# Six buffers of exponentials taken strictly in turn

## The chip, the cores and the metric

The kernel runs on one core of one Trainium2 chip. The metric is the device time in microseconds of that core, the median of three runs; lower is better.

## What is computed

The input x is 4 images of 128 channels and 64 x 64 positions, in float32. Two layers are applied. The first is a deformable 3 x 3 convolution. The second treats the 4096 positions of an image as tokens of 128 values, and has attention with 16 heads of 8 values, a small feed-forward part, and a mixture of 8 experts of which each token uses two. Cut to what matters here, the second layer is:

```python
x = x + deform_conv(group_norm(x), ...)            # layer 0
t = tokens(x)
heads = layer_norm(t).reshape(Bs, Ss, H, D)        # H = 16, D = 8
q = transpose(ring(heads + rx_theta), (0, 2, 1, 3))
scores = einsum('bhsd,bhtd->bhst', q, q) / sqrt(D)
attn = softmax(scores, axis=-1)
ctx = einsum('bhst,bhtd->bhsd', attn, q)
...                                                # projection, feed-forward, experts
```

Queries, keys and values are one and the same tensor q, so the matrix of scores is symmetric.

## The kernel before

Attention is the bulk of the work. An image has 8 chunks of 512 positions (NCH), each chunk has 4 tiles of 128 keys, and the 16 heads form 4 groups of 4 (NGRP). A *run* is one group of heads with one chunk of 512 queries; it goes over its tiles t of 128 keys. One (run, t) is a *step*. There are 3700 steps.

A step has these parts:

- `scores` (L1241): four matmuls (L1249), one a head, put the transposed scores of 128 keys and 512 queries into two PSUM tiles of the tag "sc", two heads in each. The pool of "sc" has three buffers. Two activations on ScalarE (L1258), one a PSUM tile, write the exponentials into two SBUF tiles named e, 128 x 1024 float32 each. Tag "e" has six buffers.
- `context` (L1262): the matmuls of L1266 multiply the two tiles e with the values qf (which carry a column of ones for the softmax sums) and add up in the PSUM tile acc, over all steps of a run. At the end of a run acc is copied to cu (L1468, L1470) and stored.
- `turn` (L1134): because the scores are symmetric, the exponentials of one block of queries and keys can serve, transposed, for another run. The steps that give such blocks are in the set `gives`. For them VectorE transposes both tiles e into a tile st (L1140), from where SyncE stores them to DRAM (etd, L1150). There are 396 such steps, with 792 transposes. The taking run loads them as et (L1184) and its matmuls are L1202.

So a tile e is read by PE (L1266), and in a given step by VectorE (L1140) as well. The buffer of e comes free when both are done.

The order of the main loop (L1401) is: scores of step n + 2 are issued (LAG is 2) as soon as step n is at hand; `turn` for steps n and n + 1; then a portion of the other work; then `context` of step n. On PE the scores of step s therefore stand after the context of step s - 3 and before that of step s - 2. The other work (preparing the next image, whose gathers run on GpSimd and whose convolution matmuls are L275 from L748; finishing earlier chunks with projection, feed-forward and experts) is cut into small pieces by generators. A planner, the class `Beside` (L62), puts them between the steps by its own clock of costs and due times.

The program order is kept as written for PE, VectorE, SyncE and GpSimd:

```python
with tc.manual_schedule(engines={PE, DVE, SP, POOL}):
```

ScalarE is not in that list. Its instructions are ordered, and the buffers of each tag handed out, when the program is built: the builder plays the program through and gives a tile one of the buffers of its tag that it holds to be free by then. Each instruction then gets semaphore waits for whatever its buffer's last readers are. VectorE's buffers that matter here are st (three, also used for tr, the transposed samples on their way to the DRAM table smd, L685 and L697), and v for the gathered samples.

Of the kernel before, what the change touches and what calls it, by code (L numbers as in the profile page):

```python
# [9 lines left out]
F32 = mybir.dt.float32  # L10
# [12 lines left out]
P = 128  # L23
# [195 lines left out]
def kernel(  # L219
# [29 lines left out]
    work = ctx.enter_context(tc.tile_pool(name="work", bufs=2))  # L249
# [162 lines left out]
    for i in range(NFX):  # L412
        t = big.tile([P, 4, QR], F32, name=f"fx{i}")
# [819 lines left out]
    def load_queries(run):  # L1233
        b, g, sc = runs[run][:3]
        if run not in queries and (b, sc) in prepared:
# [2 lines left out]
            queries[run] = q  # L1238
            landing[run] = beside.now + 4.0

    def scores(run, t):  # L1241
        b, g = runs[run][:2]
        ps = [
            ps_s.tile([P, 2, 512], F32, tag="sc", name=f"sc{run}_{t}_{pr}") for pr in range(2)
        ]
        kT, qT = keys[b, g, t // 4][0], queries[run]
        for i in range(4):
            h = 32 * i
            nc.tensor.matmul(  # L1249
                ps[i // 2][:, i % 2, :],  # L1250
                lhsT=kT[h : h + 32, P * (t % 4) : P * (t % 4 + 1)],
                rhs=qT[h : h + 32, :],
                start=True, stop=True,
            )
        es = []
        for pr in range(2):
            e = work.tile([P, 2, 512], F32, tag="e", name=f"e{run}_{t}_{pr}", bufs=6)
            nc.scalar.activation(e, ps[pr], AF.Exp, scale=1.0 / math.sqrt(HD))  # L1258
            es.append(e)
        return es  # L1260
# [133 lines left out]
    with tc.manual_schedule(engines={PE, DVE, SP, POOL}):  # L1394
# [6 lines left out]
        while n < len(steps):  # L1401
            if issued < len(steps) and issued <= n + LAG and at_hand(issued, n):
                es.append(scores(*steps[issued]))
                issued += 1
            elif issued <= n:
                if beside.has("prepare"):
                    beside.force("prepare")
                else:
                    beside.now += beside.STEP
                    beside.flush(beside.now)  # L1410
                continue
            run, t = steps[n]
# [137 lines left out]
```

## Time and profile before

| What | Value |
|---|---|
| Time, median of 3 runs | 7758.01 us (7747.74 to 7768.12) |
| The profiled execution's own time | 7722.51 us |
| Its span, first to last instruction | 7720.7 us |
| Mean granted TensorE clock | 0.966 |
| PE, ScalarE, VectorE, GpSimd busy | 93%, 89%, 58%, 21% of the span |
| Activations of L1258 | 7400 |
| Transposes of L1140 | 792 |

The profile is of one execution. PE is TensorE, PEld its weight loads, ACT ScalarE, DVE VectorE, POOL GpSimd, SP SyncE. Matmuls are pipelined and their ends are modelled, so a busy PE is not one at its peak. A group of instructions is named by its line, engine, operation, and the tiles that it writes and reads (acc<-e,qf), with buffer numbers left out. Behind a bar stands the time for which the engine was idle just before the group's instructions, and what ended most of that. In the list of waits a row reads: the waiting instructions, an arrow, whose end released them; then the total in us, the number of times, and the longest. In the timeline, rows run by start time; neighbours of the same line are merged, with a count.

### The profile page before, as it was taken

The page shows a single profiled execution, that of the slowest core. Times are in us where ns is not written, and L with a number is a line of the kernel's source. Part 1 is how long each engine was busy: PE and PEld are TensorE (multiplying, and loading weights), DVE is VectorE, ACT ScalarE, POOL GpSimd, SP SyncE. Part 2 cuts the span into 40 slices and gives each one's busy share as a digit, 9 for nine tenths or more (in the row PEclk, how much of TensorE's full clock was granted, in tenths as well). Part 3 has the DMA queues.
Part 4 walks back from the last instruction along what each step waited for, and adds up shares of the span by engine and source line. Part 5 has one row for each costly group of instructions (what it writes and reads, how often), then busy time and mean ns, then how long its engine had stood idle before and what let it go on. Part 6 is the DMA issues. An engine that isn't in the chain of part 4 may idle for free.

```text
span 7720.7 us, 181988 instructions
## 1 busy us (share of the span) xinstructions
PE 7154.7 (93%) x73736; PEld 2520.7 (33%) x73736; DVE 4480.6 (58%) x8976; ACT 6870.4 (89%) x7441; POOL 1655.8 (21%) x1326
## 2 busy tenths in 40 slices
PE   3589899899999999999999989989999999999997
PEld 2122233223333333333333323333333333333333
DVE  6766356666444767776444677765444545545444
ACT  0578899788999899999999988989999999999995
POOL 5544034443001332422000334431000000000000
PEclk6789999999999999999999999999999999999998
DMA  6677477978557878887766788998665587777762
GB/s 182 206 224 225 135 221 240 286 246 284 155 164 212 264 238 268 281 269 240 211 173 192 237 251 286 286 299 248 187 187 160 150 253 242 246 237 253 240 216 75
DMA packets 922615, 1730.71 MB, mean 224 GB/s; under 512 B 169074, under 2 KB 393356, under 8 KB 871084
## 3 DMA queue, kind: packets, MB, share of 16 engines
q1 hardware_dynamic: 821918, 1412.48, 60.2%
q0 software_dynamic: 92160, 302.06, 12.1%
q8 instruction: 579, 9.49, 0.5%
q10 hardware_dynamic: 7694, 4.52, 0.2%
q14 instruction: 264, 2.16, 0.1%
HBM read 1059.11 MB, written 659.57 MB: 223 GB/s over the span
## 4 chain that ended last, share of the span: by engine, by line
PE 80%; DMA 7%; DVE 4%; issue 3%; ACT 3%; SPq 2%; another core or an unknown queue 0%; POOL 0%; ACTq 0%; POOLq 0%; DVEq 0%
PE acc L1266 39%; PE sc L1249 23%; PE acc L1202 5%; PE conv_ps L275 4%; PE e_ps L275 3%; ACT e L1258 3%; PE f_ps L275 2%; DMA et<-etd 2%; DMA sT<-smd 1%; DMA etd<-st 1%; PE om_ps L530 1%; DVE v L642 1%; DVE st L1140 0%; PE ao_ps L275 0%; DMA qT<-qTd 0%
## 5 line engine op out<-in xcount | busy, mean ns | idle before, releaser
L1258 ACT ACTIVATE e<-sc 128x1024 f32<-128x1024 f32 x7400 | 6867.2, 1068 | 712.8 <-PE sc L1249 456.0
L1266 PE MATMUL acc<-e,qf 128*32 128x512 f32 x29600 | 3957.2, 605 | 18.5 <-DVE cu L1468 11.7
L1249 PE MATMUL sc<-qT,kT 32*128 32x512 f32 x14800 | 2386.7, 499 | 256.0 <-ACT e L1258 158.9
L1249 PEld LDWEIGHTS sc<-qT,kT 32*128 32x128 f32 x14800 | 954.9, 183 | 3655.4 <-ACT e L1258 3087.5
L622 POOL DMA_INDIRECT v<-tab,idx x1152 | 1453.5, 1262 | 1739.0 <-DVE tr L685 1095.4
L1140 DVE STREAM_TRANSPOSE st<-e 128x1024 f32<-128x1024 f32 x792 | 937.7, 1222 | 793.3 <-ACT e L1258 590.3
L1266 PEld LDWEIGHTS acc<-e,qf 128*32 128x32 f32 x29600 | 800.9, 110 | 580.4 <-issue 332.6
L390 POOL TENSOR_TENSOR r<-ln_t,expo 128x4 f32<-128x4 f32 x96 | 112.2, 1169 | 3134.4 <-DVE ln_t L388 3086.5
L642 DVE TENSOR_TENSOR v<-v,wt 128x1536 f32<-128x1536 f32 x384 | 665.8, 1734 | 101.3 <-DMA v<-tab,idx 78.8
L1202 PE MATMUL acc<-et,qf 128*32 128x128 f32 x12672 | 519.8, 281 | 36.4 <-DMA et<-etd 30.5
L1064 DVE TENSOR_TENSOR eo<-e_ps,gt 128x512 f32<-128x512 f32 x256 | 175.1, 686 | 546.9 <-PE e_ps L275 536.6
L1202 PEld LDWEIGHTS acc<-et,qf 128*32 128x32 f32 x12672 | 301.7, 109 | 235.2 <-issue 185.2
L275 PE MATMUL conv_ps<-sT,wconv_sb 128*32 128x256 f32 x4320 | 354.5, 401 | 25.0 <-DMA sT<-smd 19.4
L647 DVE TENSOR_TENSOR v<-v 128x768 f32<-128x768 f32 x384 | 367.4, 957 | 9.7
L1468 DVE COPY cu<-acc 128x512 f32<-128x512 f32 x128 | 88.5, 691 | 392.5 <-PE acc L1266 340.7
L685 DVE STREAM_TRANSPOSE tr<-v 128x128 f32<-128x128 f32 x1080 | 249.4, 282 | 33.1 <-DMA etd<-st 19.9
L648 DVE TENSOR_TENSOR v<-v 128x384 f32<-128x384 f32 x384 | 215.7, 562 | 13.3
L390 POOL TENSOR_TENSOR rstd<-lt_t,expo 128x4 f32<-128x4 f32 x32 | 55.7, 1741 | 523.2 <-DVE lt_t L388 514.2
L275 PE MATMUL f_ps<-w_sb,h 128*32 128x128 f32 x4096 | 165.1, 280 | 0.0
L949 DVE TENSOR_SCALAR h<-h_ps,b_sb 128x512 f32<-128x512 f32 x128 | 94.9, 743 | 102.2 <-PE h_ps L947 97.5
L822 POOL COPY fx<-rn 128x512 f32<-128x512 f32 x32 | 29.5, 923 | 531.4 <-DVE rn L821 333.8
L275 PEld LDWEIGHTS conv_ps<-sT,wconv_sb 128*32 128x32 f32 x4320 | 86.4, 109 | 162.0 <-issue 152.1
(224 smaller groups left out, 3079.3 us busy)
## 6 DMA issues: line engine op xcount, KB each, us to landing
etd<-st SPq DMA_DIRECT2D x1584, 256.0 KB
et<-etd SPq DMA_DIRECT2D x396, 1024.0 KB
kT<-kTd SPq DMA_DIRECT2D x400, 256.0 KB
smd<-tr SPq DMA_DIRECT2D x360, 192.0 KB
sT<-smd SPq DMA_DIRECT2D x360, 192.0 KB
qf<-fqd SPq DMA_DIRECT2D x400, 144.0 KB
qT<-qTd SPq DMA_DIRECT2D x166, 256.0 KB
atd<-cu SPq DMA_DIRECT2D x128, 256.0 KB
```

Of the source, the lines that this page charges most:

```text
L275: nc.tensor.matmul(dst[c : c + 32], lhsT=lhsT[:, c : c + 32], rhs=rhs, start=start, stop=stop)
L622: nc.gpsimd.indirect_dma_start(out=v[:, k, :], out_offset=None, in_=tab, in_offset=bass.IndirectOffsetOnAxis(ap=idx[:, j, kk : kk + 1], ax ...
L642: nc.vector.tensor_tensor(v4, v4, w12[:, :, None].to_broadcast([P, 12, C]), ALU.mult)
L647: nc.vector.tensor_tensor(v[:, :, : 2 * C], v[:, :, : 2 * C], v[:, :, 2 * C :], ALU.add)
L648: nc.vector.tensor_tensor(v[:, :, :C], v[:, :, :C], v[:, :, C : 2 * C], ALU.add)
L685: nc.vector.transpose(out=tr9[:, k, :, j % 4, :], in_=v[:, k, :C].rearrange("p (c i) -> p c i", i=32),)
L1064: nc.vector.tensor_tensor(ws[hf], pe.rearrange("p (e c) -> p e c", c=C), gt[:, i, 4 * hf : 4 * (hf + 1), None].to_broadcast([P, 4, C]), AL ...
L1140: nc.vector.transpose(out=st[:, :, 2 * pr : 2 * pr + 2, :].rearrange("p o h (q j) -> p o (h q) j", j=32), in_=es[pr].rearrange("p h (q o i ...
L1202: nc.tensor.matmul(acc[32 * h : 32 * (h + 1), P * kt : P * (kt + 1)], lhsT=qf[:, t, QW * h : QW * h + 32], rhs=e[:, :, h, 32 * t : 32 * (t ...
L1249: nc.tensor.matmul(ps[i // 2][:, i % 2, :], lhsT=kT[h : h + 32, P * (t % 4) : P * (t % 4 + 1)], rhs=qT[h : h + 32, :], start=True, stop=True,)
L1258: nc.scalar.activation(e, ps[pr], AF.Exp, scale=1.0 / math.sqrt(HD))
L1266: nc.tensor.matmul(acc[32 * h : 32 * (h + 1), :], lhsT=qf[:, t % 4, QW * h : QW * h + 32], rhs=es[h // 2][:, h % 2, :], start=(t == ts[0]) ...
```

## The change

A counter is kept over all tiles e. Each tile gets a tag of its own name, "e0" to "e5", by the counter modulo six, and each of the six tags has one buffer. So the tile at count k always lies where the tile at count k - 6 lay, which is three steps earlier and the same half of the step. The amount of SBUF is the same. Nothing else is changed.

```diff
+    weights_made = [0]
+
     def scores(run, t):
...
         es = []
         for pr in range(2):
-            e = work.tile([P, 2, 512], F32, tag="e", name=f"e{run}_{t}_{pr}", bufs=6)
+
+            e = work.tile([P, 2, 512], F32, tag=f"e{weights_made[0] % 6}", name=f"e{run}_{t}_{pr}", bufs=1)
+            weights_made[0] += 1
             nc.scalar.activation(e, ps[pr], AF.Exp, scale=1.0 / math.sqrt(HD))
             es.append(e)
         return es
```

## The prediction

> **What bounds the kernel now.** I read the page first, then ScalarE's waits, then two stretches of the timeline. On the page, parts 1 and 5 show two engines near their limit:
>
> ```profile
> PE 7154.7 (93%) x73736; PEld 2520.7 (33%) x73736; DVE 4480.6 (58%) x8976; ACT 6870.4 (89%) x7441; POOL 1655.8 (21%) x1326
> L1258 ACT ACTIVATE e<-sc 128x1024 f32<-128x1024 f32 x7400 | 6867.2, 1068 | 712.8 <-PE sc L1249 456.0
> ```
>
> The exponentials are 7400 activations, two a step, 3700 steps. The columns behind the bars are busy time, mean of one, and idle time ahead. ScalarE runs from 178 to 7637 us with little else than these, so what ends its 712.8 us of waits is the question. ScalarE's waits (total, times, longest):
>
> ```profile
> ACT e L1258 <- PE sc L1249: 456.0, 182, 122.5
> ACT e L1258 <- PE acc L1266: 148.5, 138, 2.7
> ...
> ACT e L1258 <- DVE st L1140: 10.7, 4, 4.9
> ```
>
> The first row is true supply: the scores were late. The second should not exist. An exponential reads scores, not acc. It can wait for the context matmul (L1266) only because that matmul still reads the buffer which the exponential is to overwrite. In PE's order, scores of step s are put down after the context of s-3 and before that of s-2. Six buffers in turn hold three steps, so the last PE reader of a buffer in turn is the context of s-3, ahead of the very scores that the exponential waits for. These 138 waits therefore mean a buffer used again after two steps. The third row is VectorE's transposes, the other reader, for the steps that are "given".
>
> The timeline shows the price. First an undisturbed step, with eight convolution matmuls beside it (columns: start, length, engine, line, operation, count, idle time before and its releaser):
>
> ```profile
> 3369.78 10.41 ACT L1258 ACTIVATE e<-sc 128x1024 f32<-128x1024 f32 x11 [0.28 <-PE sc L1249]
> ...
> 3371.11 0.50 PE L1249 MATMUL sc<-qT,kT 32*128 32x512 f32 x4
> ...
> 3371.55 0.64 PE L275 MATMUL conv_ps<-sT,wconv_sb 128*32 128x256 f32 x8
> ...
> 3372.01 1.04 PE L1266 MATMUL acc<-e,qf 128*32 128x512 f32 x8
> ...
> 3372.98 0.51 PE L1249 MATMUL sc<-qT,kT 32*128 32x512 f32 x4
> ```
>
> The step takes 3372.98 - 3371.11 = 1.87 us and ScalarE never stops: eleven activations in 10.41 us. Ten microseconds later, the same work:
>
> ```profile
> 3382.47 1.94 ACT L1258 ACTIVATE e<-sc 128x1024 f32<-128x1024 f32 x2 [1.36 <-PE acc L1266]
> 3383.54 0.19 PEld L1249 LDWEIGHTS sc<-qT,kT 32*128 32x128 f32 x2 [1.05 <-ACT e L1258]
> 3383.54 0.49 PE L1249 MATMUL sc<-qT,kT 32*128 32x512 f32 x2 [0.75 <-ACT e L1258]
> ...
> 3385.56 1.94 ACT L1258 ACTIVATE e<-sc 128x1024 f32<-128x1024 f32 x2 [1.15 <-PE acc L1266]
> 3386.63 0.18 PEld L1249 LDWEIGHTS sc<-qT,kT 32*128 32x128 f32 x2 [1.05 <-ACT e L1258]
> ```
>
> 3386.63 - 3383.54 = 3.09 us a step. It is a ring: the exponential waits for the context, the second scores wait for the exponential to empty their PSUM, the next context stands behind those scores. PE and ScalarE take turns, and both lose.
>
> **What the Trainium skill says.** "Perfetto Trace Analysis", Optimization Strategy: a gap that repeats on the engine that should be saturated can mean that there is no buffer for the next tile. The 1.15 us gaps above agree, though here six buffers are enough and the wrong one is taken. Same page, Identifying Dependency Chains: an instruction with waits on several engines may get EventSemaphore instructions ahead of it. The trace has 7393 of them, 17 ns each, before 7400 activations, so one more waiting condition adds at most such an instruction. "TensorE: Matmul & The Clock Gate", What's actually happening: an idle window of about 3.4 us halves the PE clock. The trace agrees: after a 4.28 us stop at 1713.5 us the eight context matmuls take 1.93 instead of 1.06 us.
>
> **The change, part by part.** Instructions, DMAs and their order on PE, VectorE, SyncE and GpSimd stay. Names and a counter cost nothing on the chip. Only waits of the exponentials change.
>
> *Removed:* the 138 waits on acc, 148.5 us, mean 1.08. All lie on the ring, so on the path. A second price: 3.09 - 1.87 = 1.22 us a step, times 138, is 168. A step without other matmuls gives less (2.66 at 1703 us against 1.83 at 4812 us: 0.83). I take 148.5 and keep 168 as the upper end. What is late next is PE itself, at 1.87 us a step beside 1.81 for two activations (their median spacing is 0.904).
>
> *Added:* strict turns forbid stepping around a buffer that VectorE still reads. I set the end of each of the 792 transposes (396 steps) against the start, in this trace, of the activation six places later. In 385 steps the transpose ends first: nothing is added. In eleven it ends later, by 0.05 to 9.6 us, 38.6 us together; about 1.1 us more each once the acc wait ahead is gone: 51 us. All eleven are late for a store or a load out of VectorE's own buffers:
>
> ```profile
> DVE st L1140 <- DMA etd<-st: 58.8, 14, 11.4
> DVE st L1140 <- DMA smd<-tr: 55.9, 10, 11.6
> ```
>
> But most of it was being paid already. The worst place:
>
> ```profile
> 1702.95 1.94 ACT L1258 ACTIVATE e<-sc 128x1024 f32<-128x1024 f32 x2 [0.72 <-PE acc L1266]
> ...
> 1711.12 2.37 DVE L1140 STREAM_TRANSPOSE st<-e 128x1024 f32<-128x1024 f32 x2 [11.38 <-DMA etd<-st]
> ...
> 1712.46 2.15 ACT L1258 ACTIVATE e<-sc 128x1024 f32<-128x1024 f32 x2 [4.90 <-DVE st L1140]
> ```
>
> Before, ScalarE did two more steps on short-turned buffers and then stood 4.90 us for this very transpose. After, it stands two steps earlier until the same 1712.4 and has those steps still to do: 2 x 1.86 = 3.7 us lost, not 9.4. I went through all eleven so. In seven a PE wait of 1.0 to 3.5 us on VectorE or a DMA follows within 12 us (g_ps, e_ps, conv_ps, et), and takes up the delay. The twenty short-turned steps there, worth 23.5 us in the 148.5, then bring 2.4 us lost instead: take off 26. Behind a standing activation are queued only later activations; PE waits for those two scores later.
>
> *Given back later:* after 1000 us PE's stops that do not end on an exponential are only 119 us; five follow such a stretch within 30 us outside the eleven, and eat about 1.2 us each: 6.
>
> *Unknown:* the stretches concerned have the DMA engines at 0.84 to 0.88 of their time (1000 to 1900, 2500 to 3600, 4400 to 5300 us, where 146 of the 148.5 us lie) and the same transfers must fit in 5% less. More stores will be late, each a stop of ScalarE, some long enough to halve the clock. Lower bound a gain of 10.7 us: earlier exponentials let the transposes and their stores start earlier, which can take away no more than the st row that ScalarE has now. Upper bound a loss of 89 us: the 114.7 us of the two rows above, each a stop of ScalarE in full, less the 26 counted. I take 24 lost, nearer the low end, because VectorE is only about 70% busy there and its stores start when exponentials end, so they move forward too.
>
> Sum: -148.5 + 26 + 6 + 24 = -92 us. The profiled execution took 7722.5 us (span 7720.7 and 1.8 around it), so 7630, or -1.2%. The median of the runs shown is 7758.0, 0.5% above the profiled one; the same share gives 7666.
>
> **The rivals.** (A) As above, 40 to 150 us gained. (B) The DMA engines pace the stretches: what the exponentials save comes back as stops for stores and loads, at the upper bound above: 148.5 - 26 - 6 - 89 = 27 us remain, 7731. For it: DMA shares of 0.93 to 1.00 in pieces such as 1310 to 1400 or 3110 to 3155 us. Against it: so few PE stops on DMA. (C) Slower: VectorE holds buffers and ScalarE can no longer step around. If all DMA-ended waits ahead of the transposes (164 us in the view of tile st) stop ScalarE in full and half the saving is lost otherwise, 164 - 74 = 90 us more: 7848. It decides once stops for VectorE sum to more than what the acc waits gave, that is above 0.4 us on the mean of 396 given steps; the trace has 0.1 now. (D) The buffers were in turn already, and nothing changes: 7758. The 138 waits speak against it.
>
> **How the numbers follow.** A 0.68, B 0.23, C 0.06, D 0.03. About 0.3% (23 us) is what a measurement here can tell from no change. A is faster throughout; half of B is over the bound: 0.83 faster, 0.11 same, 0.06 slower. The range goes from 7612 (146 us gained: the price of 168 with 26 and 6 off and 10.7 on) to 7732, the upper bound of the unknown; it leaves out C, D and a part of B.
>
> **What would show it.** The row of exponentials on acc L1266 should vanish, to below 10 us. The row on st L1140 should rise from 10.7 to 40 to 80. Steps of 3.09 us at 3380 us should be 1.87. PE's and ScalarE's busy shares rise a point. It is wrong if waits on acc remain (then the reuse was not their cause), if st L1140 exceeds 150 us, or if PE's stops on et, conv_ps and sT grow by as much as acc gave.

## The result and the profile after

The changed kernel takes 7828.32 us, median of 4 runs (7827.28 to 7845.88). The kernel before takes 7753.91 us over 4 runs that were made beside them. The ratio is 1.0100, interval 1.0086 to 1.0114: slower, where -1.2% was forecast. The profiled execution took 7845.9 us, with a span of 7844.1 against 7720.7 us and a mean granted clock of 0.959 against 0.966. The two profiled executions lie further apart (123 us) than the medians (74 us): the one after is the slowest of its four, and the one before is 25 us faster than any timed run of its kernel. So the traces are read for what grew and where, not for the exact size of the loss.

These are the lines of the page after that answer to those shown of before. The change added lines to the file, so the exponentials are now L1262, their scores L1251, the context matmuls L1270.

```profile
PE 7223.7 (92%) x73736; PEld 2526.2 (32%) x73736; DVE 4481.1 (57%) x8976; ACT 6880.9 (88%) x7441; POOL 1654.9 (21%) x1326
L1262 ACT ACTIVATE e<-sc 128x1024 f32<-128x1024 f32 x7400 | 6877.8, 1065 | 824.8 <-PE sc L1251 626.8
```

The work is the same in number and nearly in length. What grew is the idle time ahead of the exponentials, from 712.8 to 824.8 us. That is 112 us of the 123.4 by which the span grew; 10.6 more is their busy time (6877.8 against 6867.2). Next, ScalarE's waits in the changed kernel (total, times, longest):

```profile
ACT e L1262 <- PE sc L1251: 626.8, 377, 122.1
ACT e L1262 <- issue: 104.1, 21, 70.7
...
ACT e L1262 <- PE acc L1202: 14.8, 11, 2.6
...
ACT e L1262 <- DVE st L1140: 5.9, 4, 2.4
```

The row on acc L1266 (now L1270), 148.5 us before, is gone without a remainder. The row on st L1140, which was to rise to 40 to 80 us, fell from 10.7 to 5.9. The scores' row rose from 456.0 us in 182 waits to 626.8 in 377. One stop has changed its name and has to be put back first. It lies near the start, ends in the first row below in the kernel before and in the second in the kernel after, and is as long in both:

```profile
296.39 5.61 ACT L1258 ACTIVATE e<-sc 128x1024 f32<-128x1024 f32 x6 [70.64 <-PE sc L1249]
...
293.47 5.61 ACT L1262 ACTIVATE e<-sc 128x1024 f32<-128x1024 f32 x6 [70.68 <-issue]
```

Before, it is in the scores' row; after, it is the longest of the row "issue". Like for like, the scores' row grew from 456.0 to 697.5 us, by 241.5. So the change did take away the wait that it could take away. A larger wait for scores came up, and waits for VectorE have no part in it.

PE shows the other half. These are the rows of the context matmuls on the page before and on the page after:

```profile
L1266 PE MATMUL acc<-e,qf 128*32 128x512 f32 x29600 | 3957.2, 605 | 18.5 <-DVE cu L1468 11.7
...
L1270 PE MATMUL acc<-e,qf 128*32 128x512 f32 x29600 | 4026.2, 608 | 70.2 <-ACT e L1262 46.0
```

The idle time ahead of them grew from 18.5 to 70.2 us. PE now stops ahead of contexts because an exponential is missing, for 46.0 us, and ScalarE stops because scores are missing. Each waits for the other, though both have the same amount of work as before.

**The order on ScalarE.** A wait for scores that grows while nobody computes scores later suggests that ScalarE asks for other scores than PE delivers. So the two programs were compared, instruction by instruction. On PE, VectorE, SyncE and GpSimd the order is the same. On ScalarE it is not. Before, all 7400 exponentials stand in the order in which they are written. After, 293 of them stand elsewhere, at 60 places. The place that the timeline below shows reads thus (place among the 7400 exponentials, counted from 0, then the tile e of run, key tile and half):

```
before: 3004 e88_15_0, 3005 e88_15_1, ..., 3010 e88_29_0, 3011 e88_29_1, 3012 e88_30_0, 3013 e88_30_1, ...
after:  3004 e88_15_0, 3005 e88_15_1, ..., 3010 e88_30_0, 3011 e88_30_1, ..., 3014 e88_29_0, 3015 e88_29_1
```

The step of key tile 29 stands three steps behind that of key tile 15 and must take its two buffers. Key tile 15 is a given step: VectorE transposes those buffers too. So it is at all 60 places: the exponential that is put late takes over a buffer that a transpose (L1140) reads. At each of these places the free choice of before had stepped around that very buffer. It had done so with 124 buffers in all, each of them read by a transpose; 115 of them are those of the 115 exponentials that now come late, and the others of the 293 are moved ahead of these. In 27 of the 60, two whole steps are put ahead of a third, in the order 2, 3, 4, 5, 0, 1; the others are shorter or partly so.

The timeline of the changed kernel at this place (columns: start, length, engine, line, operation, count, idle time before and its releaser):

```profile
3465.55 1.02 ACT L1262 ACTIVATE e<-sc 128x1024 f32<-128x1024 f32 x1 [3.17 <-PE sc L1251]
...
3466.63 0.50 PE L1251 MATMUL sc<-qT,kT 32*128 32x512 f32 x2 [1.17 <-ACT e L1262]
...
3467.22 1.02 ACT L1262 ACTIVATE e<-sc 128x1024 f32<-128x1024 f32 x1 [0.65 <-PE sc L1251]
...
3468.48 0.50 PE L1251 MATMUL sc<-qT,kT 32*128 32x512 f32 x2
3469.09 1.02 ACT L1262 ACTIVATE e<-sc 128x1024 f32<-128x1024 f32 x1 [0.84 <-ACT e L1262]
...
3470.16 0.50 PE L1251 MATMUL sc<-qT,kT 32*128 32x512 f32 x2 [1.18 <-ACT e L1262]
...
3470.76 2.85 ACT L1262 ACTIVATE e<-sc 128x1024 f32<-128x1024 f32 x3 [0.65 <-PE sc L1251]
...
3472.75 2.83 PE L1270 MATMUL acc<-e,qf 128*32 128x512 f32 x8 [1.52 <-ACT e L1262]
...
3476.41 1.94 ACT L1262 ACTIVATE e<-sc 128x1024 f32<-128x1024 f32 x2 [2.80 <-PE sc L1251]
```

PE writes scores in the written order. Those of key tile 29 are done and lie in two of the three "sc" buffers. ScalarE doesn't ask for them yet, so the four score tiles of the two following steps pass one at a time through the third buffer. That is why PE's rows have x2 where an undisturbed step has x4, and why PE and ScalarE release each other in turn. The row "x3" is the last of those four exponentials and, behind it, the two of key tile 29. Their scores had been ready all along, and the context that needs them (3472.75) had stood 1.52 us. Eight exponentials take from 3465.55 to 3479.42, where the next one starts: 13.9 us.

So this is the theory: the loss is a new order of exponentials on ScalarE, which the builder chooses when a buffer is fixed by turn and it holds that buffer to be still read by VectorE. (What the builder holds is inferred from the places at which it acts.) Strict turns as such save what was forecast. The rivals: (R1) strict turns themselves cost the time, by VectorE holding the buffers, and the new order only goes with it; (R2) the free choice of before was worth something for another reason, such as that first and second halves of a step shouldn't share buffers; (R3) the time comes from elsewhere, for instance the transfers, and the displaced exponentials are too few to matter (293 of 7400).

### The profile page after: what moved, and what is told of

Read it like the earlier page. It is cut to its first block, busy times and chain, and to the rows that moved or that the text cites. A ratio compares the mean times of both kernels' runs of the same rounds, so it can differ in the third digit from the quotient of the medians.

```text
span 7844.1 us, 181706 instructions
## 1 busy us (share of the span) xinstructions
PE 7223.7 (92%) x73736; PEld 2526.2 (32%) x73736; DVE 4481.1 (57%) x8976; ACT 6880.9 (88%) x7441; POOL 1654.9 (21%) x1326
## 4 chain that ended last, share of the span: by engine, by line
PE 82%; DMA 5%; ACT 4%; DVE 4%; issue 3%; SPq 2%; another core or an unknown queue 0%; POOL 0%; ACTq 0%; POOLq 0%; DVEq 0%
PE acc L1270 40%; PE sc L1251 24%; PE acc L1202 5%; ACT e L1262 4%; PE conv_ps L275 4%; PE e_ps L275 3%; PE f_ps L275 2%; DMA et<-etd 1%; PE om_ps L530 1%; DMA sT<-smd 1%; DMA etd<-st 0%; DMA kT<-kTd 0%; PE ao_ps L275 0%; DMA qT<-qTd 0%
## 5 line engine op out<-in xcount | busy, mean ns | idle before, releaser
L1262 ACT ACTIVATE e<-sc 128x1024 f32<-128x1024 f32 x7400 | 6877.8, 1065 | 824.8 <-PE sc L1251 626.8
L1270 PE MATMUL acc<-e,qf 128*32 128x512 f32 x29600 | 4026.2, 608 | 70.2 <-ACT e L1262 46.0
L1251 PE MATMUL sc<-qT,kT 32*128 32x512 f32 x14800 | 2372.7, 501 | 277.6 <-ACT e L1262 180.6
L1251 PEld LDWEIGHTS sc<-qT,kT 32*128 32x128 f32 x14800 | 949.4, 184 | 3686.7 <-ACT e L1262 3076.6
L1140 DVE STREAM_TRANSPOSE st<-e 128x1024 f32<-128x1024 f32 x792 | 938.1, 1222 | 841.4 <-ACT e L1262 675.3
L1270 PEld LDWEIGHTS acc<-e,qf 128*32 128x32 f32 x29600 | 807.9, 110 | 682.8 <-issue 346.3
L964 DVE TENSOR_TENSOR a<-a,f_ps 128x512 f32<-128x512 f32 x32 | 22.0, 687 | 202.9 <-PE f_ps L275 202.9
```

What stands on the lines that cost most here:

```text
L1140: nc.vector.transpose(out=st[:, :, 2 * pr : 2 * pr + 2, :].rearrange("p o h (q j) -> p o (h q) j", j=32), in_=es[pr].rearrange("p h (q o i ...
L1251: nc.tensor.matmul(ps[i // 2][:, i % 2, :], lhsT=kT[h : h + 32, P * (t % 4) : P * (t % 4 + 1)], rhs=qT[h : h + 32, :], start=True, stop=True,)
L1270: nc.tensor.matmul(acc[32 * h : 32 * (h + 1), :], lhsT=qf[:, t % 4, QW * h : QW * h + 32], rhs=es[h // 2][:, h % 2, :], start=(t == ts[0]) ...
```

## The experiments

They ran in two groups on two chips. The kernel before takes 7594.06 us on the first and 7589.03 on the second (medians of 23 runs each), 2% less than in the runs above. Ratios are to these. The changed kernel itself did not run beside them; it is compared by its ratio of 1.0100, and the second group is compared with the kernel with ties of the first by ratio too. Both take for granted that ratios carry over from chip to chip.

**Turns kept, the written order kept.** Each exponential is tied behind the one written before it. Nothing else is written differently from the changed kernel. With the ties, the order on every engine is that of the kernel before, instruction by instruction, and only the buffers of the tiles e differ from it. So against the kernel before this run tests strict turns alone. Against the changed kernel it tests the order, with one thing that follows from it: the builder hands out the three "sc" buffers too, and in the changed program 5219 of the 7400 score tiles got another one than before and than here.

```diff
+    weights_last = []
...
-            nc.scalar.activation(e, ps[pr], AF.Exp, scale=1.0 / math.sqrt(HD))
+            made = nc.scalar.activation(e, ps[pr], AF.Exp, scale=1.0 / math.sqrt(HD)).ins
+            if weights_last and True:
+                tc.add_manual_dep(made, weights_last[0].name, mybir.DependencyInfo(mybir.DependencyClass.NoSync, mybir.DependencyReason.DATA), reason="order")
+            weights_last[:] = [made]
```

> The changed kernel with one thing more: every exponential on ScalarE is tied behind the one written before it, so that ScalarE's order is the written order again. In the changed kernel 293 of the 7400 exponentials stand out of that order, at 60 places. Theory 1 (the loss is ScalarE's new order): the time falls to what the prediction's sum gave, 7662 us (7612 to 7732), 0.988 of before; no row of exponentials on acc, exponentials on the transposes L1140 wait 40 to 80 us, those on sc fall back to about 456 us from 627. Theory 2 (the loss is VectorE holding the buffers, the order only steps around it): with the order held ScalarE must stand for VectorE, the row on L1140 is over 150 us, and the time stays at 7800 us or more.

Measured: 7500.55 us (7489.21 to 7510.31), ratio 0.9868, interval 0.985 to 0.9885. That is faster than before by 1.3% and than the change by 2.3%. ScalarE's waits in this kernel:

```profile
ACT e L1263 <- PE sc L1252: 436.9, 85, 120.9
ACT e L1263 <- DVE st L1140: 72.4, 14, 12.7
```

There is no row on acc, and the scores' row is down to 85 waits. The row on st, 72.4 us, is now what the prediction had asked for, 40 to 80 us. And this is the timeline of the same steps in this kernel:

```profile
3242.04 14.80 ACT L1263 ACTIVATE e<-sc 128x1024 f32<-128x1024 f32 x16 [0.20 <-ACT e L1263]
...
3244.97 0.50 PE L1252 MATMUL sc<-qT,kT 32*128 32x512 f32 x4
...
3245.40 0.64 PE L275 MATMUL conv_ps<-sT,wconv_sb 128*32 128x256 f32 x8
...
3245.86 1.04 PE L1274 MATMUL acc<-e,qf 128*32 128x512 f32 x8
...
3246.83 0.50 PE L1252 MATMUL sc<-qT,kT 32*128 32x512 f32 x4
```

Sixteen exponentials run without a stop and a step takes 1.86 us. The eight that took 13.9 us take 7.3. The buffer that the builder had held to be busy was free in time here. R1 falls for the loss, and R3 falls too: the order, with the score buffers that follow from it, is the only difference and it is worth 2.3%. R2 falls as well, since strict turns beat the free choice once the order is the same.

**The order written down.** The same by another way: ScalarE is added to the engines whose program order is kept as written.

```diff
+ACT = mybir.EngineType.Activation
...
-    with tc.manual_schedule(engines={PE, DVE, SP, POOL}):
+    with tc.manual_schedule(engines={PE, DVE, SP, POOL, ACT}):
```

> The changed kernel with ScalarE put on the list of engines whose whole program order is kept, which also moves four small activations (L556, L1016) by one to three places and fixes ScalarE's DMA issues. Theory 1: the same as with the tied exponentials, 7662 us, within 0.3%. Theory 2: 7800 us or more.

Measured: 7501.49 us, ratio 0.9875 (0.9857 to 0.9893), the same as with the ties. The gain isn't a side effect of the ties. ScalarE's waits in this kernel are much the same too:

```profile
ACT e L1263 <- PE sc L1252: 413.2, 83, 118.8
ACT e L1263 <- DVE st L1141: 76.9, 15, 11.9
```

**Turns kept, the order held in the third image only.** The condition of the tie is `if weights_last and b == 2`. This undoes 26 of the 60 places, with 123 of the 293 displaced exponentials.

> The changed kernel with ScalarE's order tied as in the run above, but in the third image alone: 26 of the 60 places and 123 of the 293 displaced exponentials are in it. Theory 1: the gain is in proportion, 123/293 of the 166 us between 7828 and 7662, so 7758 us, 1.000 of before, and in the trace only the third image gets shorter. Theory 2: 7800 us or more.

Measured: 7604.32 us, ratio 1.0011 (1.0002 to 1.002), against 1.000 expected. The time from one image's first exponential to the next one's shows where it was won. In the third image it is 1803.6 us, where the kernel with all ties has 1812.6; in the second, which is left to the builder, it is 1817.2 against 1757.4. (The kernel with halves in turn, below, which takes the time of before, has 1840.4 and 1793.8.) The gain is in the image whose order is held and nowhere else.

**The order held at the 27 longest places only.** The tie is made only for the exponentials at the 27 places at which two whole steps were put ahead of a third; 32 other places remain in that program.

> The changed kernel with the written order tied only at the 27 places where three steps were permuted; 32 places and 127 displaced exponentials remain, nearly all of two steps. By the two traces those 27 places hold 140 of the 188 us. Theory 1: 48 us remain over the order-held kernel, 0.993 of before. Theory 2: 1.00 or more.

Measured: 7553.04 us, ratio 0.9953 (0.9936 to 0.9969), against 0.993 expected. From 1.0100 to 0.9953 is 1.5 of the 2.3 points. The 32 places that are left cost 0.9953 - 0.9868 = 0.0085 of 7589, 65 us (48 were expected) or 2 us each, and the 27 long ones the other 112 us, or 4 us each. The long ones are the dear ones.

**The same misorder, put where there was none.** The kernel with ties is tied in another order: at 60 places, evenly spaced in the last image (exponentials 5600 to 7257), whose time the change had left nearly as it was (1722.3 us against 1719.5), the order is 2, 3, 4, 5, 0, 1. The diff is against the changed kernel. The turns and buffers of e are the same.

```diff
+    acts, chained = [], []
+    asked = list(range(7400))
+    for at in range(5600, 7280, 28):
+        asked[at : at + 6] = [at + 2, at + 3, at + 4, at + 5, at, at + 1]
...
-            nc.scalar.activation(e, ps[pr], AF.Exp, scale=1.0 / math.sqrt(HD))
+            acts.append(nc.scalar.activation(e, ps[pr], AF.Exp, scale=1.0 / math.sqrt(HD)).ins)
+            while asked and asked[0] < len(acts):
+                if chained:
+                    tc.add_manual_dep(acts[asked[0]], chained[-1].name, mybir.DependencyInfo(mybir.DependencyClass.NoSync, mybir.DependencyReason.DATA), reason="order")
+                chained.append(acts[asked.pop(0)])
```

> The order-held kernel with the displaced order put in by hand at 60 places in the last image (exponentials 5600 to 7257, one in 28), where the changed kernel has hardly any: the exponentials of steps s+1 and s+2 ahead of those of s. No buffer is late there. Theory 1 (order alone costs): each place costs what the places of this shape cost in the changed kernel's trace against the order-held one, median 6.9 us (mean 5.2), so 60 of them 310 to 410 us on top of 0.987: 1.028 to 1.041 of before. Theory 2 (order costs only where VectorE or its stores are late anyway): 0.987 to 0.992.

Measured: 7909.05 us, ratio 1.0422 (1.0404 to 1.0439), a little above the upper end of 1.041 that was expected. Against the kernel with ties that is (1.0422 - 0.9868) x 7589 = 420 us, or 7.0 us a place. ScalarE's waits, and below them PE's for exponentials, in this kernel:

```profile
ACT e L1266 <- PE sc L1255: 796.2, 390, 120.8
...
ACT e L1266 <- DVE st L1140: 67.7, 12, 11.1
...
PE acc L1278 <- ACT e L1266: 102.3, 60, 2.1
```

The scores' row has 305 waits and 359 us more than with the written order, about five waits a place. The row on st is the same. PE's contexts stand for exponentials 60 times, once a place. It is the changed kernel's signature, and the order alone makes it.

With half the places (`range(5600, 7272, 56)`):

> The same with every second place left out, 30 places. Theory 1: half of the addition, 1.007 to 1.014 of before. Theory 2: 0.987 to 0.990.

Measured: 7708.33 us, ratio 1.0154 (1.0133 to 1.0175): (1.0154 - 0.9868) x 7589 = 217 us, or 7.2 us for each of 30. The upper end of the expectation was 1.014, so this lies a little above. The cost grows with the number of places.

**Turns for each half, the choice left free.** First halves of a step use three buffers, second halves three others; within the three the builder chooses.

```diff
-            e = work.tile([P, 2, 512], F32, tag=f"e{weights_made[0] % 6}", name=f"e{run}_{t}_{pr}", bufs=1)
+            e = work.tile([P, 2, 512], F32, tag=f"e{weights_made[0] % 2}", name=f"e{run}_{t}_{pr}", bufs=3)
```

> Six buffers under two names, one for each half of a step, three buffers each, and among the three the free choice as before. In its program 282 exponentials wait for a context later than their scores (281 before) and none stands out of order. Theory 1: as before, 1.000 within 0.3%, 7754 us, with 140 to 150 us of waits on acc, since neither names nor a fixed half cost anything. Theory 2 (naming buffers takes VectorE's freedom away): slower by 0.3 to 1%.

Measured: 7590.84 us, ratio 0.9997 (0.9988 to 1.0005): no difference from before. ScalarE's waits in this kernel:

```profile
ACT e L1262 <- PE sc L1251: 403.0, 77, 121.1
ACT e L1262 <- PE acc L1270: 157.5, 143, 2.7
...
ACT e L1262 <- DVE st L1140: 14.8, 4, 6.6
```

The row on acc has come back with the free choice. So it isn't the mixing of halves that makes buffers be used again after two steps, it is stepping around a buffer. This trace also serves as the kernel before on the chip of the first group.

**Turns and written order, scores only one step ahead.** In the kernel with ties, LAG is 1 instead of 2. The six buffers then have one step more in which to come free, but PE has one step less in hand.

> The order-held kernel with LAG 1 instead of 2: scores of s come after the context of s-2, so a buffer in turn has a step more before it is needed again. An attempt at a faster version. If VectorE's late buffers are what is left (72 us of waits on L1140), they fall below 30 us and the time goes to about 0.98 of before. If ScalarE needs the two steps of lead, PE waits for exponentials and the time goes above 1.0. I hold the second for likelier.

Measured: 7584.76 us, ratio 0.999 (0.9983 to 0.9997). ScalarE's waits in this kernel:

```profile
ACT e L1263 <- PE sc L1252: 522.0, 173, 120.1
...
ACT e L1263 <- DVE st L1140: 36.0, 11, 8.0
```

The expectation was missed on both sides: the row on st fell by half but not below 30 us, and the time came out neither below the kernel with LAG 2 nor above the kernel before. What the slack for VectorE gave back (36 us) was outweighed by later scores (85 us more).

## Why the prediction was wrong

**The step that failed** is the first sentence of the change part by part: "Instructions, DMAs and their order on PE, VectorE, SyncE and GpSimd stay", followed by "Only waits of the exponentials change". The first is true of the four engines that it names. The second doesn't follow, for there is a fifth: ScalarE is the engine that the program leaves to the builder, and the exponentials are on it. The change gave the builder another question. With a free choice it had kept the exponentials in order and chosen a buffer; with the buffer fixed it kept the buffer and chose the order. I had quoted that ScalarE isn't on the list and still counted its order as given. "Behind a standing activation are queued only later activations" fails for the same reason.

**The waits on acc**, 148.5 us to be removed: right, and right about the cause. The row is gone with strict turns in both orders and back (157.5 us) with a free choice. What I hadn't seen is that the 138 waits and the 60 displaced places are two answers to one belief of the builder's, that VectorE's transposes end later than they do on the chip. The count above supports it (115 of the 124 buffers stepped around are those of the displaced exponentials); the belief itself is inferred.

**The VectorE stops**, 26 us net and 24 us for the unknown: with the ties, the row on st is 72.4 us, inside the 40 to 80 that were named, and 57.6 more than the 14.8 of the kernel that stands for before on that chip. The 26 us are what was left after stops that the kernel before had already paid elsewhere, so no row shows them alone. In the changed kernel there is nothing of it (5.9 us), presumably because the displaced exponentials give VectorE more time.

**Given back later**, 6 us: not settled. Between the same two traces the scores' row grows by 436.9 - 403.0 = 34 us, but in the kernel with the order written down it grows by 413.2 - 403.0 = 10 us only. One execution of each doesn't tell 6 from either. Between the first two the waits come to -157.5 + 57.6 + 34 = -66 us, and the span falls by 69.6. The forecast sum of -1.2% lies inside what the ties give over all runs, -1.3% (-1.5 to -1.15), so the sum for strict turns was right, though its smaller terms are known only in part.

**The term that was missing** is the order. By ratios it is (1.0100 - 0.9868) x 7754 = 180 us, or 3.0 us at each of 60 places. Counted directly in the traces of the two kernels, which are of two chips, over the stretches of these places, from two exponentials ahead of each to seven behind, it is 1006.2 - 818.1 = 188 us. With other margins it comes to between 160 and 220. Part of it is the clock. The mean granted clock fell from 0.966 to 0.959, and by the clock records the changed kernel is at half speed for 647 us and the kernel before for 532. If half speed doubles what PE does meanwhile, up to 57 of the 123 us between these two traces are the clock's; this is an estimate, and no run separates it from the waits.

**The rivals.** C (slower, 7848 us) came near in number, and it was wrong in its mechanism: it was to decide once stops for VectorE sum to more than the acc waits gave, and they sum to 5.9 us. B falls with it, and with the ties the forecast gain came in full, which B had denied. D falls, since the buffers had not been in turn. The statement of what would make the prediction wrong named three rows (acc, st, and PE's own loads), and the loss is in none of them. The chances given don't add up as stated: 0.68 and half of 0.23 are 0.80 for faster and not 0.83, and the same half with D's 0.03 makes 0.15 for the same and not 0.11. The spacing of 0.904 us between exponentials holds for those that run straight on; the median over all of them is 0.92.

**What stays open.** Why the builder holds the transposes to be later than the chip shows was not tried. The misorder with freely chosen buffers was not tried either, nor the misorder with the score buffers held as they were, nor seven or eight buffers.

## What to carry to other kernels

Before pricing a change of buffers or tags, list which engines have a written order and which are left to the builder, and compare the instruction order of the two programs on the latter before reading any wait. Two engines that hand tiles to each other through few buffers must agree on the order: here a producer in written order, a consumer two steps off and three PSUM tiles cost 7 us a time where they were put at odds by hand, and about 3 us a time in the changed kernel. A fixed turn of buffers is worth having where the reuse distance was too short (1.3% here), but here it paid only together with the fixed order.

## What the runs showed of the hardware

I hadn't expected the PE clock to fall at so short stops. The Trainium skill, "TensorE: Matmul & The Clock Gate", What's actually happening, tells of an idle window of about 3.4 us that halves the clock. These are two adjoining stretches of the kernel with 60 misplaced steps, around the first of them (columns: window, its us, busy time of PE, PEld, DVE, ACT and POOL with counts, granted PE clock, DMA share, GB/s):

```profile
5731.40:5738.60 7.20, 3.42 (x30) 1.13 (x30) 0.01 (x1) 5.05 (x6) 0.00 (x0) 0.93 0.26 94
5738.60:5745.00 6.40, 6.39 (x32) 1.46 (x32) 3.34 (x4) 2.81 (x3) 0.00 (x0) 0.55 0.49 107
```

In the first, PE is busy for 3.42 of 7.20 us, in pieces; the timeline there has its longest stops as follows:

```profile
5732.49 0.50 PE L1255 MATMUL sc<-qT,kT 32*128 32x512 f32 x2 [1.18 <-ACT e L1266]
...
5736.02 0.50 PE L1255 MATMUL sc<-qT,kT 32*128 32x512 f32 x2 [1.17 <-ACT e L1266]
...
5738.61 2.84 PE L1278 MATMUL acc<-e,qf 128*32 128x512 f32 x8 [1.53 <-ACT e L1266]
...
5742.97 1.73 PE L1278 MATMUL acc<-e,qf 128*32 128x512 f32 x8
```

None is longer than 1.53 us. The records put the clock at half speed at 5737.5 us, for 6.8 us, and the eight context matmuls at 5742.97 take 1.73 us instead of 1.04. (In the 2.84 us of the row above it is also a wait for the second exponential.) So no stop as long as 3.4 us was needed here. From 5731 to 7400 us this kernel is at half speed for 256 us in 44 pieces; the kernel with the written order, over the same work, for 3.4 us in one. The pieces begin and end on a grid of 3.41 us. In the 3.41 us ahead of each of the 44, PE was busy for 0.20 to 0.67 of the time, and the longest stop there was 2.1 us. Not every such stretch with 0.55 or more was followed by half speed, so the records give no threshold. If half speed doubles all that PE does in these 44 pieces, it is up to 128 of the 420 us. No run separates it from the waits, so the share is an estimate and stays open. The place of the first timeline, in the changed kernel, has it too: half speed from 3471.9 us for 6.8 us.
